# Layer 0 of a two-layer graph network: the normalised rows transposed by the DMA crossbar as two planes of 16 bits, and the head products placed among the next node tile's products

## The chip, the cores and the metric

The kernel runs on one core of a Trainium2 chip. A core has five engines, each with an instruction stream of its own that is executed in order: TensorE (PE, matmuls and transposes into PSUM), VectorE (DVE), ScalarE (ACT), GpSimd (POOL) and SyncE (SP). Here SP issues the loads and POOL the stores. Engines wait for each other through semaphores. The metric is the device time of one launch in microseconds, as the median of the runs; lower is better.

## The reference

There are 3327 nodes with 1024 features each, and a dense adjacency matrix of 3327 x 3327 with mostly zeros. Layer 0 quantises the normalised rows and the weights, multiplies them, and then multiplies by the adjacency matrix. Layer 1 is a graph attention with 8 heads of 64 features and a small dense network behind it. Both are residual. Cut to what matters here:

```python
h = jnp.maximum(_layernorm(x), 0.0)
x = x + _L0_gnn_ref(h, adj, ...)     # output = adj @ support_q, rescaled
h = jnp.maximum(_layernorm(x), 0.0)
Wh = jnp.einsum('nf,hfd->hnd', h, W)        # 1024 features -> 8 heads x 64
e_src = jnp.einsum('hnd,hd->hn', Wh, a1)
e_dst = jnp.einsum('hnd,hd->hn', Wh, a2)
e = jnp.where(adj > 0, leaky_relu(e_src[:, :, None] + e_dst[:, None, :], 0.2), NEG)
att = jax.nn.softmax(e, axis=-1)
x = x + mlp(elu(einsum('hnm,hmd->hnd', att, Wh)))
```

The change concerns the fourth line and the normalisation above it: the product of the normalised rows of `x` after layer 0 with the head weights `W`.

## The kernel before

The nodes are cut into 26 tiles of 128 (`T`). The kernel has four parts: the quantised product of layer 0 (`s_int`, one tile of 128 x 1024 for each node tile, all kept in SBUF), the adjacency product of layer 0 (lines 433 to 460), the attention, and the dense network.

The adjacency product is the part at hand. For each node tile `t` there are 104 matmuls of 128x128 by 128x512 (line 444): 26 column blocks `j`, two halves of the output, and two summands `hi` and `lo` of the adjacency block, which is split so that two rounded products add up to the exact one. The column blocks come in four parts of 7, 6, 7 and 6 (`PARTS`). `adjacency` (lines 172 to 189) loads a part (`at`, 3 buffers), makes `hi` on ScalarE (line 179) and `lo` on VectorE (line 183), each with 2 buffers, and the mask of non-zeros (`mk`, line 184). A part is asked for one part ahead of its products.

When a tile's products are done, ScalarE reads them out of PSUM (`y`, line 452), VectorE rescales them (line 453), adds the old rows (`xt`, line 454), and `normalised` computes mean and variance, then the inverse deviation (`inverse_std`, lines 127 to 137), and writes `(xt - mean) * r` to `y` (line 152). POOL stores `xt`.

`heads(t, h)` then works on the normalised tile: TensorE transposes its eight blocks of 128 x 128 (line 381), ScalarE copies them to `ht` with a ReLU (line 382), TensorE multiplies them by the head weights (line 385, eight float32 matmuls that show as sixteen in the trace), ScalarE copies the product (`wht`, line 387), VectorE forms the two attention terms `src` and `dst` (lines 392 and 393), TensorE transposes `src` (line 399), and ScalarE and VectorE build the features `ft`, `fw` and `dw`, which POOL stores for the attention. `heads` is called one tile late: after the products of tile `t` and its normalisation, the heads of tile `t - 1` are worked on, and the heads of the last two tiles follow the loop.

A scheduler sets the order of the instructions on each engine, moving them within what the data allow; `tc.keep_in_program_order` pins an instruction to where it is written. In the order that it made, the eight transposes of tile `t - 1` stand right behind the products of tile `t`, then five products of tile `t + 1`, then the head matmuls, ten products, the transpose of `src`, and the other 89 products. SP's queue holds the `at` loads, four to a tile, and one load of old rows `xt` (line 125). At the end of the part, the loads of the attention (masks, `f_even`, `dw`, `srow`) follow in the same queue.

Of the kernel before, what the change touches and what calls it, by code (L numbers as in the profile page):

```python
# [8 lines left out]
F32 = mybir.dt.float32  # L9
BF16 = mybir.dt.bfloat16  # L10
F32R = mybir.dt.float32r
U8 = mybir.dt.uint8
I8 = mybir.dt.int8
AF = mybir.ActivationFunctionType
ALU = mybir.AluOpType
# [4 lines left out]
P = 128  # L20
N = 3327
T = (N + P - 1) // P
NP = T * P
TH = T // 2
F = 1024
KF = F // P
# [9 lines left out]
EPS = 1e-5  # L36
# [23 lines left out]
def two_layer_kernel(  # L60
# [23 lines left out]
    nc = tc.nc  # L84
# [5 lines left out]
    ident = const.tile([P, P], F32, name="ident")  # L90
# [7 lines left out]
    x1_d = dram.tile([NP, F], F32, name="x1_d")  # L98
    mask_d = dram.tile([T, P, T, P], U8, name="mask_d")
    feat_d = dram.tile([T, NH, P, HW], F32, name="feat_d")  # L100
# [26 lines left out]
    def inverse_std(var, n, eps, tag):  # L127

        v, s, r, q = (small.tile([P, n], F32, tag=tag + c, name=tag + c) for c in "vsrq")
        nc.vector.tensor_scalar(v, var, eps, None, ALU.add)  # L130
        nc.scalar.activation(s, v, AF.Sqrt)
        nc.vector.reciprocal(r, s)
        nc.vector.tensor_tensor(q, v, r, ALU.mult)
        nc.vector.tensor_tensor(q, q, s, ALU.add)
        nc.vector.tensor_scalar(q, q, 0.5, None, ALU.mult)
        nc.vector.reciprocal(r, q)
        return r
# [7 lines left out]
    def normalised(dst, src):  # L145

        stats = small.tile([P, FC, 6], F32, tag="stats", name="stats")
        statistics(stats, src)
        mv = small.tile([P, 2], F32, tag="mv", name="mv")
        nc.vector.bn_aggr(mv, stats.rearrange("p c s -> p (c s)"))  # L150
        r = inverse_std(mv[:, 1:2], 1, EPS, "ln")
        nc.vector.tensor_scalar(dst, src, mv[:, 0:1], r, ALU.subtract, ALU.mult)

    def normaliser(mv, n, eps, factor, tag):

# [12 lines left out]
    with tc.tile_pool(name="wh", bufs=1, reuse_waits="tile") as whp, tc.tile_pool(  # L168
        name="at", bufs=2, reuse_waits="tile"
# [56 lines left out]
        with tc.tile_pool(name="s1", bufs=2, reuse_waits="tile") as s1, tc.tile_pool(  # L226
            name="s1_tp", bufs=2, space=PSUM, reuse_waits="tile"
# [81 lines left out]
            for c in range(FC):  # L309
                r = slice(c * 512, (c + 1) * 512)  # L310
# [16 lines left out]
            whead = whp.tile([P, KF, EMB], F32, name="whead")  # L327
# [43 lines left out]
        with tc.tile_pool(name="s2", bufs=2, reuse_waits="tile") as s2, tc.tile_pool(  # L371
            name="s2_tp", bufs=2, space=PSUM, reuse_waits="tile"
        ) as tp_ps, tc.tile_pool(name="s2_wh", bufs=2, space=PSUM, reuse_waits="tile") as wh_ps:

            def heads(t, h):
                ht = s2.tile([P, KF, P], F32, name="ht", bufs=1)
                for g in range(KF // 4):
                    tp = tp_ps.tile([P, 4, P], F32, tag="tp2", name="tp2")
                    for q in range(4):
                        k = 4 * g + q  # L380
                        nc.tensor.transpose(tp[:, q, :], h[:, k * P : (k + 1) * P], ident)
                    nc.scalar.activation(ht[:, 4 * g : 4 * g + 4, :], tp, AF.Relu)  # L382
                whm = wh_ps.tile([P, EMB], F32, name="whm")
                for k in range(KF):
                    nc.tensor.matmul(whm, ht[:, k, :], whead[:, k, :], start=(k == 0), stop=(k == KF - 1))  # L385
                wht = s2.tile([P, EMB], F32, name="wht", bufs=1)
                nc.scalar.copy(wht, whm)
                src = small.tile([P, NH], F32, name="src")
                dst = small.tile([P, NH], F32, name="dst")
                for a_t, e in ((a1_t, src), (a2_t, dst)):  # L390
                    prod = s2.tile([P, EMB], F32, name="prod", bufs=1)
                    nc.vector.tensor_tensor(prod, wht, a_t, ALU.mult)
                    nc.vector.tensor_reduce(
                        e, prod.rearrange("p (h d) -> p h d", d=HD), AX.X, ALU.add
                    )
                nc.vector.tensor_scalar(ndst[:, t], dst, -1.0, None, ALU.mult)
                nc.scalar.activation(ratio[:, t], src, AF.Exp, scale=1.0 - SLOPE)
                sp = tp_ps.tile([P, 4, P], F32, tag="tp2", name="sp")
                nc.tensor.transpose(sp[:NH, 0, :], src, ident)
                srct = s2.tile([NH, P], F32, name="srct")  # L400
                nc.scalar.copy(srct, sp[:NH, 0, :])
                for sub, d in zip(SUBS, src_d):
                    if t in sub:
                        nc.gpsimd.dma_start(d[:, (t - sub[0]) * P : (t - sub[0] + 1) * P], srct)

                ft = s2.tile([P, NH, 2, HC], F32, name="ft", bufs=1)
                wh3 = wht.rearrange("p (h d) -> p h d", d=HD)
                for q, slope in enumerate((1.0, SLOPE)):
                    nc.scalar.activation(ft[:, :, q, HD], dst, AF.Exp, scale=slope)
                    nc.vector.tensor_tensor(  # L410
                        ft[:, :, q, :HD], wh3, ft[:, :, q, HD:].to_broadcast([P, NH, HD]), ALU.mult
                    )
                fw = s2.tile([P, NH, 2, 2 * HC], F32R, name="fw", bufs=1)
                f2 = ft.rearrange("p h q c -> p h (q c)")
                nc.scalar.copy(fw[:, :, 0], f2)
                nc.vector.tensor_tensor(fw[:, :, 1], f2, fw[:, :, 0].bitcast(F32), ALU.subtract)

                dw = s2.tile([P, NPAIR, 2, 2, HC], F32R, name="dw", bufs=1)
                for q in range(2):
                    nc.scalar.copy(  # L420
                        dw[:, :, q],
                        fw[:, :, q, HC:].bitcast(F32).rearrange("p (g e) c -> p g e c", e=2),
                    )
                nc.gpsimd.dma_start(
                    feat_d[t].rearrange("h p c -> p h c"),
                    fw.bitcast(F32).rearrange("p h q c -> p h (q c)"),
                )
                nc.gpsimd.dma_start(
                    dsum_d[t].rearrange("g p c -> p g c"),
                    dw.bitcast(F32).rearrange("p g q e c -> p g (q e c)"),  # L430
                )

            before = None
            for t in range(T):
                xt = s2.tile([P, F], F32, name="xt2")
                load_rows(xt, x, t)
                mm = mm_ps.tile([P, F], F32, tag="mm", name="mm2")
                for js in PARTS:
                    hi, lo = part
                    part = next(columns, None)  # L440
                    for q, j in enumerate(js):
                        for which in (hi, lo):
                            for c in range(FC):
                                nc.tensor.matmul(  # L444
                                    mm[:, c * 512 : (c + 1) * 512],
                                    which[:, q, :],
                                    s_int[j][:, c * 512 : (c + 1) * 512],
                                    start=(j == 0 and which is hi),
                                    stop=(j == T - 1 and which is lo),
                                )  # L450
                y = s2.tile([P, F], F32, name="y")
                nc.scalar.activation(y, mm, AF.Copy, scale=r_asf)
                nc.vector.tensor_scalar(y, y, asf_t, sup_delta, ALU.mult, ALU.mult)
                nc.vector.tensor_tensor(xt, xt, y, ALU.add)
                nc.gpsimd.dma_start(x1_d[t * P : (t + 1) * P, :], xt)
                normalised(y, xt)
                if before is not None:
                    heads(*before)
                before = (t, y)
            heads(*before)  # L460
    supp.close()

# [23 lines left out]
    with tc.tile_pool(name="f1", bufs=1, reuse_waits="tile") as f1p, tc.tile_pool(  # L486
        name="sel", bufs=4, reuse_waits="tile"
    ) as selp, tc.tile_pool(name="srow", bufs=2, reuse_waits="tile") as srowp, tc.tile_pool(name="mf", bufs=2, reuse_waits="tile") as mfp, tc.tile_pool(
        name="md", bufs=2, reuse_waits="tile"
    ) as mdp, tc.tile_pool(name="s3", bufs=1, reuse_waits="tile") as s3, tc.tile_pool(  # L490
        name="s3_acc", bufs=7, space=PSUM, reuse_waits="tile"
# [142 lines left out]
        for i, (c, g, e, si) in enumerate(attends):  # L634
# [75 lines left out]
            h = 2 * g + e  # L710
            sub, mask = halves[c][si], masks[si]
            nb = len(sub)
            f = f_odd if e else f_even
            srow_next = load_src(i + 1) if i + 1 < len(attends) else None
            accs = [acc_ps.tile([P, HW], F32, tag="acc", name="acc") for _ in sub]
            for j in range(T):
                n = i * T + j
                k, m = divmod(n - 20, 2 * T)
# [41 lines left out]
    with tc.tile_pool(name="s4", bufs=2, reuse_waits="tile") as s4, tc.tile_pool(  # L760
        name="s4_ps", bufs=4, space=PSUM, reuse_waits="tile"
# [22 lines left out]
        for g, t0 in enumerate(range(0, T, 4)):  # L784
# [7 lines left out]
            else:  # L792
                enct = s4.tile([P, EMB // P, 512], F32, name="enct")
                for k in range(EMB // P):
                    tp = ps_p.tile([P, 512], F32, tag="ps", name="tp4")
# [8 lines left out]
            for q, t in enumerate(tiles):  # L804
                nc.vector.tensor_tensor(x1[:, q, :], x1[:, q, :], bb4, ALU.add)
                ps = o_ps.tile([P, F], F32, name="o")
                for c in range(FC):
                    for k in range(D3 // P):
# [4 lines left out]
                            start=(k == 0),  # L813
                            stop=(k == D3 // P - 1),
# [50 lines left out]
```

## Time and profile before

| | us |
|---|---|
| median of 3 runs | 2292.01 |
| lowest and highest | 2291.98, 2293.26 |
| the profiled execution, its time | 2293.44 |
| the profiled execution, its span | 2291.7 |
| adjacency product, from the first `y` to the last (170.9 to 957.5) | 786.6 |

The granted TensorE clock was 0.995 of full speed. Rows of the profile read thus: a group of instructions has its line, engine, operation, what it writes and reads, shapes and count, then the busy time of the group and the mean duration of one, then the idle time of the engine just before them and what ended it. Matmuls are pipelined, so their means overlap; the distance between two starts is the price of one. A row of a timeline has start, duration, and in brackets the idle time before it. A row of a stage has its busy time and instruction counts of PE, PEld (weight loads, beside PE), DVE, ACT and POOL, then the granted clock, the busy share of the DMA engines and GB/s. A row of DMA issues has the size and the median time from issue to landing.

### The profile page before, as it was taken

To read this page: it belongs to the slowest core of one execution; us is meant where nothing else is said; L and a number is where in the kernel's file an instruction comes from. 1 tells how busy PE (TensorE), PEld (TensorE's weight loads), DVE (VectorE), ACT (ScalarE), POOL (GpSimd) and SP (SyncE) were. 2 spreads that over 40 slices of the span, in tenths; PEclk is the share of its full clock that TensorE was granted. 3 is DMA by queue.
4 is the path that set the end of the run, shared out by engine and by line. 5 is a ranking of instruction groups with operands and counts; after the bars stand their busy time and mean duration, and the time that the engine had idled before them with its cause. 6 is when DMAs were issued, how large, how long until landed. Compare 5 with 4: busy or idle time off the path is not lost. (4 is left out here: it accounts for less than half of the span.)

```text
span 2291.7 us, 32041 instructions
## 1 busy us (share of the span) xinstructions
PE 2233.5 (97%) x12896; PEld 1785.0 (78%) x12896; DVE 1559.1 (68%) x2090; ACT 998.2 (44%) x1654; POOL 119.3 (5%) x173
## 2 busy tenths in 40 slices
PE   4999999999999999889999999999999999999999
PEld 2467777777777777579999999999999999744444
DVE  7845555555555555487999999999999999732211
ACT  4753333333333333346555555555555555411120
POOL 0000110111101111000000000000000000000000
PEclk9999999999999999999999999999999999999999
DMA  6324444444445444763324142654242422343311
GB/s 234 129 82 149 151 150 142 162 145 155 151 141 162 151 149 152 239 210 118 99 73 134 45 142 80 215 178 154 84 144 77 141 87 75 112 152 123 125 55 55
DMA packets 150301, 304.94 MB, mean 133 GB/s; under 512 B 10172, under 2 KB 91020, under 8 KB 150152
## 3 DMA queue, kind: packets, MB, share of 16 engines
q1 hardware_dynamic: 130248, 229.72, 30.3%
q0 software_dynamic: 19904, 73.17, 9.9%
q8 instruction: 101, 1.65, 0.3%
q14 instruction: 48, 0.39, 0.1%
HBM read 216.07 MB, written 86.79 MB: 132 GB/s over the span
## 5 line engine op out<-in xcount | busy, mean ns | idle before, releaser
L729 DVE SCALAR_TENSOR_TENSOR sel<-srow,ndst,mask 128x896 fp32r<-128x896 f32 (+1 forms) x832 | 864.1, 1079 | 54.4 <-PE acc L738 41.2
L539 PE MATMUL mps<-dw,mf 128*128 128x260 f32 x2704 | 453.3, 283 | 0.1
L444 PE MATMUL mm<-s_int,hi 128*128 128x512 f32 x1352 | 433.0, 399 | 0.0
L444 PE MATMUL mm<-s_int,lo 128*128 128x512 f32 x1352 | 421.6, 391 | 0.0
L738 PE MATMUL acc<-f_even,sel 128*128 128x260 f32 x2704 | 396.9, 284 | 1.4 <-DVE sel L729 1.1
L738 PE MATMUL acc<-f_odd,sel 128*128 128x260 f32 x2704 | 395.0, 286 | 0.0
L538 ACT CAST mf<-mask 128x1664 fp32r<-128x1664 uint8 x208 | 331.3, 1593 | 123.5 <-PE mps L539 100.2
L539 PEld LDWEIGHTS mps<-dw,mf 128*128 128x128 f32 x2704 | 377.7, 188 | 0.3 <-ACT part L543 0.3
L738 PEld LDWEIGHTS acc<-f_odd,sel 128*128 128x128 f32 x2704 | 353.4, 188 | 7.3 <-issue 3.1
L738 PEld LDWEIGHTS acc<-f_even,sel 128*128 128x128 f32 x2704 | 354.9, 188 | 5.4 <-DVE sel L729 2.8
L444 PEld LDWEIGHTS mm<-s_int,lo 128*128 128x128 f32 x1352 | 253.8, 188 | 57.6 <-issue 5.7
L444 PEld LDWEIGHTS mm<-s_int,hi 128*128 128x128 f32 x1352 | 252.1, 188 | 55.6 <-issue 5.7
L184 DVE TENSOR_SCALAR mk<-at 128x896 uint8<-128x896 f32 x104 | 61.7, 594 | 267.1 <-DMA at<-in_adj_t 266.1
L179 ACT CAST hi<-at 128x896 fp32r<-128x896 f32 x104 | 92.7, 891 | 328.8 <-PE mm L444 294.8
L385 PE MATMUL whm<-whead,ht 128*128 128x512 f32 x416 | 186.7, 602 | 0.8 <-ACT ht L382 0.8
L809 PE MATMUL o<-weights,h 128*128 128x512 f32 x416 | 179.7, 592 | 0.0
L809 PEld LDWEIGHTS o<-weights,h 128*128 128x128 f32 x416 | 79.0, 190 | 99.1 <-issue 99.0
L385 PEld LDWEIGHTS whm<-whead,ht 128*128 128x128 f32 x416 | 77.4, 191 | 98.0 <-issue 87.8
L183 DVE TENSOR_TENSOR lo<-at,hi 128x896 fp32r<-128x896 f32 x104 | 106.6, 1025 | 49.0 <-ACT hi L179 38.8
L543 ACT COPY part<-mps 128x260 f32<-128x260 f32 x104 | 39.3, 378 | 223.9 <-PE mps L539 223.9
L819 DVE TENSOR_TENSOR yo<-o,nodes 128x1024 f32<-128x1024 f32 (+1 forms) x27 | 31.8, 1182 | 139.2 <-PE o L809 139.2
L333 PE MATMUL mm<-w_int,xqt 128*128 128x512 bf16 x416 | 97.7, 386 | 10.2 <-DVE w_int L319 7.7
(136 smaller groups left out, 1567.8 us busy)
## 6 DMA issues: line engine op xcount, KB each, us to landing
feat_d<-fw POOLq DMA_DIRECT2D x26, 1040.0 KB, 5.3
f_even<-feat_d SPq DMA_DIRECT2D x7, 3380.0 KB, 13.1
f_odd<-feat_d SPq DMA_DIRECT2D x7, 3380.0 KB, 12.3
at<-in_adj_t SPq DMA_DIRECT2D x52, 448.0 KB, 4.2
at<-in_adj_t SPq DMA_DIRECT2D x52, 384.0 KB, 3.2
mask<-mask_d SPq DMA_DIRECT2D x39, 416.0 KB, 6.9
dw<-dsum_d SPq DMA_DIRECT2D x16, 910.0 KB, 8.9
dsum_d<-dw POOLq DMA_DIRECT2D x26, 520.0 KB, 6.5
```

The lines of the kernel that those rows point to most:

```text
L179: ins = nc.scalar.copy(hi, at)
L183: nc.vector.tensor_tensor(lo, at, hi.bitcast(F32), ALU.subtract)
L184: nc.vector.tensor_scalar(mk[:, r], at, 0.0, None, ALU.is_gt)
L333: nc.tensor.matmul(mm[:, c * 512 : (c + 1) * 512], xqts[t][:, k, :], w_int[:, k, c * 512 : (c + 1) * 512], start=(k == 0), stop=(k == KF - 1),
L385: nc.tensor.matmul(whm, ht[:, k, :], whead[:, k, :], start=(k == 0), stop=(k == KF - 1))
L444: nc.tensor.matmul(mm[:, c * 512 : (c + 1) * 512], which[:, q, :], s_int[j][:, c * 512 : (c + 1) * 512], start=(j == 0 and which is hi), s ...
L538: nc.scalar.copy(mf, mask[:, j : j + TH, :])
L539: nc.tensor.matmul(ps, mf[:, j % TH, :], dw[:, j, :], start=(j == 0), stop=(j == T - 1))
L543: nc.scalar.copy(part[:, i % 7], ps.rearrange("p (q c) -> p q c", q=2))
L729: nc.vector.scalar_tensor_tensor(sel[:, :nb], srow[:, :nb], ndst[:, j, h : h + 1], mask[:, :, j, :], ALU.is_gt, ALU.mult,)
L738: nc.tensor.matmul(accs[b], sel[:, b, :], f[:, j, :], start=(j == 0), stop=(j == T - 1))
L809: nc.tensor.matmul(ps[:, c * 512 : (c + 1) * 512], h3[:, k, q * P : (q + 1) * P], w4[:, k, c * 512 : (c + 1) * 512], start=(k == 0), stop= ...
```

## The change

Four things are changed.

- Tiles 0 to 24 are transposed by a DMA on SP's queue. ScalarE first copies `y` into two planes of 16 bits (`yh`: all lower halves of the float32 words, then all upper halves), the DMA transposes 128 rows by 2048 columns into sixteen blocks (`yht`), and ScalarE copies the planes back into float32 words (`ht`). The last tile is transposed by TensorE as before.
- The transposition is asked for right after the tile's normalisation.
- The heads of tile `t - 1` are called within the products of tile `t`, after column block 16, and their first matmul is pinned there.
- `normalised` writes `max(xt - mean, 0)` and hands the inverse deviation `r` on. As `r` is positive and one number for each row, it is multiplied in later, where `heads` reads its product out of PSUM (`wht`).

`y` has one buffer instead of two.

```diff
+U16 = mybir.dt.uint16
@@ normalised
-        r = inverse_std(mv[:, 1:2], 1, EPS, "ln")
-        nc.vector.tensor_scalar(dst, src, mv[:, 0:1], r, ALU.subtract, ALU.mult)
+        nc.vector.tensor_scalar(dst, src, mv[:, 0:1], 0.0, ALU.subtract, ALU.max)
+        return inverse_std(mv[:, 1:2], 1, EPS, "ln")
@@ adjacency product
-            def heads(t, h):
+            def halves_of_words(words):
+
+                return words.bitcast(U16).rearrange("p (n two) -> p two n", two=2)
+
+            def transposed_by_dma(y):
+
+                yh = s2.tile([P, 2, F], U16, name="yh", bufs=1)
+                nc.scalar.copy(yh, halves_of_words(y))
+                yht = s2.tile([P, 2 * KF, P], U16, name="yht", bufs=1)
+                nc.sync.dma_start_transpose(yht, yh.rearrange("p two f -> p (two f)"))
+                ht = s2.tile([P, KF, P], F32, name="ht", bufs=1)
+                nc.scalar.copy(
+                    halves_of_words(ht.rearrange("p k i -> p (k i)")),
+                    yht.rearrange("p (two k) i -> p two (k i)", two=2),
+                )
+                return ht
+
+            def transposed_by_tensor(y):
                 ht = s2.tile([P, KF, P], F32, name="ht", bufs=1)
                 for g in range(KF // 4):
                     tp = tp_ps.tile([P, 4, P], F32, tag="tp2", name="tp2")
                     for q in range(4):
                         k = 4 * g + q
-                        nc.tensor.transpose(tp[:, q, :], h[:, k * P : (k + 1) * P], ident)
-                    nc.scalar.activation(ht[:, 4 * g : 4 * g + 4, :], tp, AF.Relu)
+                        nc.tensor.transpose(tp[:, q, :], y[:, k * P : (k + 1) * P], ident)
+                    nc.scalar.copy(ht[:, 4 * g : 4 * g + 4, :], tp)
+                return ht
+
+            def heads(t, ht, r):
                 whm = wh_ps.tile([P, EMB], F32, name="whm")
                 for k in range(KF):
-                    nc.tensor.matmul(whm, ht[:, k, :], whead[:, k, :], start=(k == 0), stop=(k == KF - 1))
+                    ins = nc.tensor.matmul(
+                        whm, ht[:, k, :], whead[:, k, :], start=(k == 0), stop=(k == KF - 1)
+                    )
+                    if k == 0:
+                        tc.keep_in_program_order(ins)
                 wht = s2.tile([P, EMB], F32, name="wht", bufs=1)
-                nc.scalar.copy(wht, whm)
+                nc.scalar.activation(wht, whm, AF.Copy, scale=r)
@@ the loop over node tiles
+                        if j == 16 and before is not None:
+                            heads(*before)
-                y = s2.tile([P, F], F32, name="y")
+                y = s2.tile([P, F], F32, name="y", bufs=1)
...
-                normalised(y, xt)
-                if before is not None:
-                    heads(*before)
-                before = (t, y)
+                r = normalised(y, xt)
+                before = t, (transposed_by_tensor if t == T - 1 else transposed_by_dma)(y), r
             heads(*before)
```

## The prediction

> **What bounds the kernel now.** I read the page first (which engine is full), then busy time by stage, then the groups of the stage that the diff touches, then its timelines.
>
> ```profile
> PE 2233.5 (97%) x12896; PEld 1785.0 (78%) x12896; DVE 1559.1 (68%) x2090; ACT 998.2 (44%) x1654; POOL 119.3 (5%) x173
> ...
> 234.00:957.00 723.00, 723.00 (x2940) 530.59 (x2939) 382.38 (x627) 268.87 (x407) 76.06 (x113) 1.00 0.47 153
> 957.00:990.00 33.00, 19.63 (x56) 9.43 (x54) 16.44 (x28) 10.66 (x19) 2.79 (x4) 0.84 1.00 348
> ```
>
> In the second part of layer 0 (234 to 957 us) TensorE is busy for all 723 us; VectorE 382, ScalarE 269, DMA engines at 0.47. Only PE's work, or a wait on PE, counts there. The 33 us at its end are different: PE busy for 20, DMA share 1.00 at 348 GB/s.
>
> ```profile
> L385 PE MATMUL whm<-whead,ht 128*128 128x512 f32 x416 | 186.7, 602 | 0.8 <-ACT ht L382 0.8
> L381 PE MATMUL tp<-ident,y 128*128 128x128 f32 x208 | 27.8, 278 | 0.3 <-DVE y L152 0.3
> ```
>
> The 208 transposes (8 for each of 26 node tiles) hold PE for 27.8 us; 200 of them go. Means overlap, so their price is better read from starts, PE's timeline of one tile:
>
> ```profile
> 511.61 0.62 PE L444 MATMUL mm<-s_int,lo 128*128 128x512 f32 x2
> 512.07 1.03 PE L381 MATMUL tp<-ident,y 128*128 128x128 f32 x8
> 512.86 0.71 PE L444 MATMUL mm<-s_int,hi 128*128 128x512 f32 x2
> ...
> 513.86 0.39 PE L444 MATMUL mm<-s_int,hi 128*128 128x512 f32 x1
> 514.20 7.13 PE L385 MATMUL whm<-whead,ht 128*128 128x512 f32 x16
> 520.77 0.79 PE L444 MATMUL mm<-s_int,hi 128*128 128x512 f32 x1
> ```
>
> Products start every 0.227 us (two in 0.46). The eight transposes take 512.86 - 512.07 = 0.79; the step from the last product to the heads is 0.34 instead of 0.23, PE waiting 0.11 for `ht`; and the 16 head matmuls (0.43 a start) contain one more such wait of about 0.1. Sum 1.0 us a tile. The period comes from the starts of `y` (ScalarE's timeline):
>
> ```profile
> 170.89 1.11 ACT L452 ACTIVATE y<-mm,r_asf 128x1024 f32<-128x1024 f32 x1
> ...
> 194.46 1.11 ACT L452 ACTIVATE y<-mm,r_asf 128x1024 f32<-128x1024 f32 x1
> ...
> 512.54 1.11 ACT L452 ACTIVATE y<-mm,r_asf 128x1024 f32<-128x1024 f32 x1
> ...
> 544.36 1.11 ACT L452 ACTIVATE y<-mm,r_asf 128x1024 f32<-128x1024 f32 x1
> ```
>
> A tile with heads in it is 31.82 us; tile 1, which has none before the change, 23.57.
>
> [...]
>
> **The change part by part.** S is the start of a tile's first product; it lies 0.47 us before `y` (512.07 to 512.54).
>
> *Removed.* 1.0 us of PE in each of 25 tiles; the two 0.59 us reads of the transposed PSUM on ScalarE (hidden). A tile with heads becomes 31.8 - 1.0 = 30.8, plus a wait w if `ht` is late.
>
> *Moved.* In the program's order the 16 head matmuls stand after 68 of the tile's 104 products, so PE reaches them at S + 68 x 0.2265 = S + 15.4. They now belong to the previous tile, so tile 1 has heads too, and only the last tile's heads remain behind the loop. Loop before: 786.6 us (170.9 to 957.5). After: 25 x 30.8 = 770 + 25w. That is -16.6 + 25w.
>
> *The new chain, from PE's end to `ht`.* VectorE's part of it, in the second tile shown (S = 543.9):
>
> ```profile
> 545.51 0.81 DVE L453 TENSOR_SCALAR y<-y,every,sup_delta 128x1024 f32<-128x1024 f32 x1
> 546.35 1.23 DVE L454 TENSOR_TENSOR xt<-xt,y 128x1024 f32<-128x1024 f32 x1
> 547.61 1.29 DVE L141 BATCH_NORM_STATS2 stats<-xt 128x6 f32<-128x512 f32 x2
> ...
> 549.71 0.20 DVE L150 BATCH_NORM_AGGREGATE mv<-stats 128x2 f32<-128x12 f32 x1
> ```
>
> There the first `y` starts at S+1.6. In the new order one mask comparison more (0.56) stands ahead of it: S+2.1. Then 0.84 + 1.26 + 1.32, another comparison 0.55, 0.24, and the subtract-and-max at the price of the old normalisation, 0.81: 5.0, so `y` is ready at S+7.1. The inverse deviation is off this path, since it now scales `wht`. On ScalarE `hi` of part 2 stands before `yh`; it waits for PE's part 0 (S + 28 x 0.227 = 6.3 at the latest) and takes 0.95, so it is out of the way at about 7.1. `yh` has 2048 elements a partition: 1040 take 1.06 us (`fw`) and 520 take 0.63 (`dw`), that is 0.83 ns an element and 0.2 fixed: 1.9. [...] It ends at S+9.0.
>
> *The DMA.* SP's order is `xt` of the next tile, the transpose, then the next `at` loads: behind the waiting transpose stand only loads for the next tile, wanted over 10 us later, and ahead of it a 512 KB load that starts about S+7.5. The trace's nearest transfers:
>
> ```profile
> xt<-in_x SPq DMA_DIRECT2D x25, 512.0 KB, 3.2
> enc_d<-ht POOLq DMA_DIRECT2D x16, 224.0 KB, 3.1
> enc_d<-ht POOLq DMA_DIRECT2D x16, 192.0 KB, 2.8
> ```
>
> If as fast as a regular 512 KB, X = 3.2 us. If it goes by pieces of 256 bytes, as `enc_d` does (7 x 128 pieces in 3.1, 6 x 128 in 2.8: 0.3 per 128), 2048 pieces give 3.1 + 9 x 0.3 = 5.8. [...] I take 4.5, the middle of the two values from this trace. `ht` is another 1.9 us of ScalarE, with `hi` of part 3 ahead of it, which is done at about S+12.9, before the data. So `ht` ends at S + 9.0 + 4.5 + 1.9 + 0.3 for hand-overs = S+15.7: w = 15.7 - 15.4 = 0.3, in all 7.5 us. Behind `ht` on ScalarE wait only the heads' own work and then `hi` of the next tile's part 0. In the trace `ft` ends 4.4 us after the last head product (520.8 to 525.2); `hi` (0.95) and `lo` (1.1) make 6.5, while PE has 36 products (8.2 us) left: covered by 1.7 us.
>
> *The end of the stage.* Before, the heads of tile 24 and 25 both follow the loop, and PE stands for the transpose of `src`:
>
> ```profile
> PE sp L399 <- DVE src L393: 12.1, 2, 9.9
> ```
>
> VectorE was waiting for loads with four `sel` queued ahead of `prod`. From the last `y` (957.5) to the first attention product (989.4) is 31.9 us. After: `y` ready 5.6 us after the last product, tensor transposes and copies to 7.3, heads to 14.3; `srow`, behind two more `dw` pieces but started 7 us earlier against the loop's end, lands at about 11.4, four `sel` to 15.9, `prod` and its sum to 17.5, attention at 18. That is -14; I take -12, for the transpose of tile 24 now shares the queue with three mask loads (416 KB each). If the stretch stays bound by its DMA, as the share of 1.00 allows, it is only -3.
>
> Sum: -16.6 + 7.5 - 12 = -21. The profiled run took 2293.4 us with a span of 2291.7, the median is 2292.0; the difference of 0.06% is below anything argued here. 2292 - 21 = 2271.
>
> **The rivals.** With w = 0 the whole is worth 28.6 us, 1.14 a tile. So the change turns into a loss where the transposing DMA takes over 4.5 - 0.3 + 1.14 = 5.35 us, or the two copies together take 0.84 us more than I took at 4.5.
>
> *A. In time or nearly so* (X from 3.2 to 5.2): 2263 to 2288, forecast 2271. For it: [...] DMA engines at 0.47. Against: pieces of 256 bytes, and `xt` just ahead in the queue.
>
> *B. The transposing DMA is late, and PE waits for `ht` in each tile; slower.* One mechanism: PE executes in order, so the whole of X beyond 5.35 is lost 25 times over. By the pieces' price of 5.8, w = 1.6: 40 - 28.6 = +11, 2303. At 8 us, w = 3.8: +66, 2358. [...] For it: [...] the `enc_d` rows. Against: nothing in this trace moves 512 KB so slowly without a queue ahead of it.
>
> *C. It cancels* (X about 5.2 to 5.5): 2292.
>
> *D. The loop gains, the end doesn't*: -16.6 + 7.5 - 3 = -12, 2280; it lies within A. That the transposes stay on PE is excluded: in the new order only the last tile's eight are left.
>
> **How the numbers follow.** A (with D) 0.55, C 0.05, B 0.40, of which 0.25 up to X = 8.7 and 0.15 above. What this kernel's measurement can tell from no change is about 0.2%, 4.6 us. Faster 0.55, same 0.05, slower 0.40. A's own range is 2260 to 2288. The range on record reaches from 2258 (no wait, the end at its best, and 0.1 us a tile for the rounding of 1.0) to 2375 (X = 8.7), leaving out the far end of B.
>
> **What would show it.** Right: `y` to `y` at 30.8 to 31.2 us; `yht` landing within 5 us of its issue; head matmuls preceded by less than 0.5 us of PE idle; first attention product about 18 us after the last `y`. Wrong: PE idle before `whm` put down to ACT `ht`, of over 1.1 us a tile; `yh` or `ht` well above 1.9 us; PE waiting at the start of a tile for `hi` or `lo`. A landing time over 5.35 us alone would turn the sign.

## The result, and the profile after

| | before | after |
|---|---|---|
| median | 2292.11 us (4 runs) | 2397.49 us (4 runs) |
| lowest and highest | 2291.98, 2293.26 | 2387.61, 2399.82 |
| the profiled execution: time, span | 2293.44, 2291.7 | 2395.86, 2393.8 |
| granted clock over the span | 0.995 | 0.975 |
| adjacency product, first `y` to last | 786.6 | 902.2 |
| last `y` to the first attention product | 31.8 | 18.9 |
| from there to the end of the span | 1302.3 | 1302.3 |

The ratio is 1.045, with an interval of 1.042 to 1.048: slower, where faster had been forecast. All of it lies in the adjacency product: +115.6 us there, -13.0 at its end, nothing behind. ScalarE's timeline has the two ends of the loop (start, duration):

```profile
170.48 1.11 ACT L479 ACTIVATE y<-mm,r_asf 128x1024 f32<-128x1024 f32 x1
...
1072.65 1.11 ACT L479 ACTIVATE y<-mm,r_asf 128x1024 f32<-128x1024 f32 x1
```

25 periods in 902.2 us are 36.1 us each; before, a tile with heads took 31.8, and 30.8 plus a wait of 0.3 was forecast. The groups of the changed instructions, PE's and ScalarE's:

```profile
L406 PE MATMUL whm<-whead,ht 128*128 128x512 f32 x416 | 228.7, 713 | 86.3 <-ACT ht L387 86.3
L399 PE MATMUL tp<-ident,y 128*128 128x128 f32 x8 | 2.0, 428 | 5.8 <-DVE lnv L131 5.8
L387 ACT COPY ht<-yht 128x2048 uint16<-128x2048 uint16 x25 | 61.6, 2466 | 59.5 <-DMA yht<-yh 59.5
L383 ACT COPY yh<-y 128x2048 uint16<-128x2048 uint16 x25 | 47.5, 1899 | 71.7 <-DVE y L152 71.7
```

200 transposes are gone, as intended. In their place PE stands for 86.3 us ahead of the head products, waiting for ScalarE's copy `ht`, and the head products themselves are busy for 228.7 us instead of 186.7. The transposing DMA is not what is slow (the view of the tile `yht`: durations of the issue in ns, min/median/max, then the times to landing):

```profile
L385 SPq DMA_TRANSPOSE yht<-yh x25: 1798/1942/3491, 178.9 to 1049.5; - x25
...
DMA to landing us min/median/max: 4.2/4.3/6.6
```

So PE waits, but the transfer takes 4.3 us in the median, no more than the 4.5 that were taken for it. Most of the time must be lost before it. One tile shows where; its first product starts at S = 574.31. First POOL's timeline (DMA issues; start, duration, and in brackets the wait before):

```profile
573.77 0.93 POOL L449 DMA_DIRECT2D feat_d<-fw  x1 [4.24 <-DVE fw L441]
574.69 0.77 POOL L453 DMA_DIRECT2D dsum_d<-dw  x1
578.62 0.55 POOL L482 DMA_DIRECT2D x_d<-xt  x1 [3.15 <-DVE xt L481]
```

SP's:

```profile
584.09 0.33 SPq L126 DMA_DIRECT2D xt<-in_x  x1
586.03 3.14 SPq L385 DMA_TRANSPOSE yht<-yh  x1
```

VectorE's:

```profile
578.35 1.29 DVE L142 BATCH_NORM_STATS2 stats<-xt 128x6 f32<-128x512 f32 x2
582.53 0.63 DVE L185 TENSOR_SCALAR mk<-at 128x896 uint8<-128x896 f32 x1 [2.89 <-DMA at<-in_adj_t]
583.08 0.20 DVE L151 BATCH_NORM_AGGREGATE mv<-stats 128x2 f32<-128x12 f32 x1
583.31 0.75 DVE L152 TENSOR_SCALAR y<-xt,mv 128x1024 f32<-128x1024 f32 x1
```

ScalarE's:

```profile
584.10 1.90 ACT L383 COPY yh<-y 128x2048 uint16<-128x2048 uint16 x1 [2.88 <-DVE y L152]
...
591.22 2.46 ACT L387 COPY ht<-yht 128x2048 uint16<-128x2048 uint16 x1 [2.98 <-DMA yht<-yh]
```

PE's:

```profile
589.14 0.61 PE L469 MATMUL mm<-s_int,lo 128*128 128x512 f32 x2
593.73 9.94 PE L406 MATMUL whm<-whead,ht 128*128 128x512 f32 x16 [3.97 <-ACT ht L387]
603.11 1.02 PE L469 MATMUL mm<-s_int,hi 128*128 128x512 f32 x2
```

Between the statistics and the mean VectorE has a mask comparison `mk` in its queue, and waits 2.89 us for the adjacency load `at` that it reads. This load is issued at S+1.6, while the two stores of the previous tile's heads (`feat_d` 1040 KB, `dsum_d` 520 KB, issued at S-0.5 and S+0.4) are on the DMA engines, and lands 6.5 us later; the load at the same place of the tile of before landed after 3.9. There the heads' stores went out late in the tile, at S+17.9 (S = 512.07, POOL's timeline of before):

```profile
529.95 0.93 POOL L424 DMA_DIRECT2D feat_d<-fw  x1 [5.02 <-DVE fw L416]
```

`y` is ready at S+9.8, forecast S+7.1. From there the chain runs nearly as forecast: `yh` 1.90, DMA 5.17 (this tile is slower than the median of 4.3), `ht` 2.46, PE at S+19.4 instead of S+15.4. And the 16 head products then take 603.11 - 593.73 = 9.4 us instead of the 6.57 (514.20 to 520.77) of before.

The stages view in slices of about 8 us, for this tile and for the tile of before that the prediction used. Columns: PE, PEld, DVE, ACT and POOL busy, granted clock, DMA share, GB/s. Before, from S = 512.07:

```profile
512.07:520.07 8.00, 8.00 (x28) 4.39 (x27) 6.08 (x13) 4.04 (x6) 1.10 (x2) 1.00 0.52 177
520.07:528.07 8.00, 8.00 (x34) 5.84 (x34) 5.98 (x11) 4.29 (x8) 0.53 (x1) 1.00 0.19 67
528.07:536.07 8.00, 8.00 (x37) 6.64 (x36) 3.11 (x4) 2.38 (x4) 1.70 (x2) 1.00 0.74 237
536.07:543.90 7.83, 7.83 (x37) 6.41 (x36) 1.83 (x3) 1.23 (x2) 0.00 (x0) 1.00 0.40 123
```

After, from S = 574.31:

```profile
574.31:582.31 8.00, 8.00 (x37) 6.63 (x36) 4.66 (x6) 2.53 (x3) 2.25 (x4) 1.00 0.92 303
582.31:590.31 8.00, 7.45 (x33) 5.82 (x31) 4.23 (x11) 4.11 (x4) 0.00 (x0) 1.00 0.89 220
590.31:598.31 8.00, 4.58 (x6) 2.00 (x7) 1.19 (x2) 2.46 (x1) 0.00 (x0) 0.64 0.34 109
598.31:606.31 8.00, 8.00 (x25) 4.30 (x24) 1.81 (x3) 2.28 (x4) 0.00 (x0) 0.93 0.00 0
606.31:612.08 5.77, 5.77 (x27) 4.76 (x26) 4.66 (x7) 3.79 (x8) 1.07 (x2) 1.00 0.19 51
```

Read the DMA column downwards. Before, the third slice had the most (0.74): there the heads' stores went out. After, they sit in the first slice, and the first two are at 0.92 and 0.89, just where the chain to `ht` needs its loads and its transfer; from 594 to 606 the DMA engines are nearly empty. The mean share over the loop is 0.49, as before (0.47), and tells nothing of this.

The clock column is the second finding. The same view around the wait:

```profile
592.30:593.70 1.40, 0.00 (x0) 0.00 (x0) 0.02 (x1) 1.38 (x1) 0.00 (x0) 0.60 0.87 353
593.70:598.70 5.00, 4.97 (x6) 2.19 (x7) 1.17 (x2) 0.00 (x0) 0.00 (x0) 0.50 0.01 4
598.70:603.10 4.40, 4.40 (x11) 1.88 (x10) 0.00 (x0) 0.00 (x0) 0.00 (x0) 0.92 0.00 0
```

After the wait of 3.97 us PE runs for 5 us at a granted clock of 0.50, and then for 4.4 us at 0.92; in the last 1.4 us of the wait it is at 0.60 already. That the lower clock belongs to the waits is shown by e6 below: there PE waits 0.9 us in all, the clock over the loop is 1.00, and the head products are busy for 185.2 us, against 186.7 before the change and 228.7 here. What makes the clock fall and come back, and after how long, was not shown; how long the waits were that had slow head products behind them is in the last section.

Together: 86.3 us of waiting and about 43 us of slow head products (228.7 against the 185.2 of a later version that doesn't wait) are about 130 of the 132 us by which the loop is longer than its 770 without waits.

### The profile page after: what moved, and what is told of

Read it like the earlier page. It is cut to its first block, busy times and chain, and to the rows that moved or that the text cites. A ratio compares the mean times of both kernels' runs of the same rounds, so it can differ in the third digit from the quotient of the medians.

```text
span 2393.8 us, 31681 instructions
## 1 busy us (share of the span) xinstructions
PE 2254.0 (94%) x12684; PEld 1779.3 (74%) x12696; DVE 1548.7 (65%) x2090; ACT 1082.5 (45%) x1656; POOL 118.5 (5%) x173
## 5 line engine op out<-in xcount | busy, mean ns | idle before, releaser
L469 PE MATMUL mm<-s_int,hi 128*128 128x512 f32 x1352 | 427.0, 397 | 0.0
L406 PE MATMUL whm<-whead,ht 128*128 128x512 f32 x416 | 228.7, 713 | 86.3 <-ACT ht L387 86.3
L406 PEld LDWEIGHTS whm<-whead,ht 128*128 128x128 f32 x416 | 93.1, 230 | 211.1 <-issue 114.1
L417 DVE TENSOR_TENSOR prod<-wht,a_t 128x512 f32<-128x512 f32 x52 | 36.0, 692 | 225.8 <-ACT wht L412 224.9
L412 ACT ACTIVATE wht<-whm,lnr 128x512 f32<-128x512 f32 x26 | 17.9, 688 | 230.3 <-PE whm L406 230.3
```

The costliest lines, as they stand in the source:

```text
L406: ins = nc.tensor.matmul(whm, ht[:, k, :], whead[:, k, :], start=(k == 0), stop=(k == KF - 1))
L469: nc.tensor.matmul(mm[:, c * 512 : (c + 1) * 512], which[:, q, :], s_int[j][:, c * 512 : (c + 1) * 512], start=(j == 0 and which is hi), s ...
```

## The experiments

These lines allow two theories. The mask theory says that the loss is the mask comparison alone, which stands ahead of the mean and waits for a late load. The store theory says that the heads' stores, moved into the first microseconds of the tile, fill the DMA engines, and that the comparison is only one of several things that wait. Each expectation names its own theories. A third question was whether the placing of the heads in the products costs anything by itself. All of them are compared with before; "loop" is the adjacency product from the first `y` to the last, and "PE idle" is summed over all tiles:

| run | median, us | ratio (95%) | loop | PE idle before `whm` |
|---|---|---|---|---|
| changed kernel | 2397.49 | 1.045 (1.042 to 1.048) | 902.2 | 86.3 |
| e1: mask made from `hi` | 2394.67 | 1.0433 (1.0407 to 1.0459) | 904.3 | 91.4 |
| e4: heads after block 18 | 2299.38 | 1.0032 (1.0020 to 1.0044) | 809.3 | 26.8 |
| e3: e1 and e4 together | 2317.50 | 1.0111 (1.0096 to 1.0126) | 826.7 | 40.0 |
| e2: TensorE transposes, heads moved | 2284.71 | 0.9967 (0.9954 to 0.9980) | 792.3 | 0.0 |
| e5: stores late, on SP's queue | 2293.09 | 1.0007 (0.9999 to 1.0016) | 800.3 | 24.2 |
| e8: stores late, on POOL's queue | 2303.37 | 1.0043 (1.0028 to 1.0058) | 809.5 | 30.0 |
| e9: stores early, on SP's queue | 2418.64 | 1.0544 (1.0526 to 1.0561) | 924.0 | 90.1 |
| e6: e5 and heads after block 18 | 2262.45 | 0.9872 (0.9856 to 0.9889) | 769.7 | 0.9 |
| e7: heads two tiles late | 2283.68 | 0.9966 (0.9953 to 0.9979) | 778.8 | 0.2 |

**e1: the mask comparison doesn't wait for the load.**

```diff
-            nc.vector.tensor_scalar(mk[:, r], at, 0.0, None, ALU.is_gt)
+            nc.vector.tensor_scalar(mk[:, r], hi.bitcast(F32), 0.0, None, ALU.is_gt)
```

> The changed kernel with one edit: the comparison mk reads hi in place of at, so on VectorE it can no longer stand before the mean and variance and wait there for the load of the next tile's part 0. Theory A (the heads come late mainly because y waits behind that comparison, whose load lands 6.5 us after its issue beside the stores of feat_d and dsum_d): y is ready at S+6.5 to 7.2 instead of S+9.8 (S: the tile's first product), yh ends at about 9.1, the transpose lands at 13.4, ht ends at 15.9, PE waits under 1.0 us before the heads, the 16 head products take 6.54 us from first to last start instead of 8 to 9.6, a tile takes 31.2 to 31.6 us instead of 36.4, and the time is 2270 to 2290. Rival B (the transposing DMA and its copies are too long by themselves): the wait stays above 3 us and the time above 2370. Rival C (the lower granted clock comes from something other than the waits): the wait shrinks, but head products still take over 8 us in most tiles, 2310 to 2340.

Nothing came of it: 2394.67. The corresponding tile starts at S = 570.10. VectorE's timeline:

```profile
575.84 0.75 DVE L152 TENSOR_SCALAR y<-xt,mv 128x1024 f32<-128x1024 f32 x1
```

SP's:

```profile
580.92 0.33 SPq L126 DMA_DIRECT2D xt<-in_x  x1
581.35 3.94 SPq L385 DMA_TRANSPOSE yht<-yh  x1
```

ScalarE's:

```profile
577.84 1.89 ACT L383 COPY yh<-y 128x2048 uint16<-128x2048 uint16 x1
588.27 2.46 ACT L387 COPY ht<-yht 128x2048 uint16<-128x2048 uint16 x1 [6.47 <-DMA yht<-yh]
```

`y` is ready at S+6.5, 3.3 us earlier than in the changed kernel, and `yh` at S+9.6. But SP issues the transposing DMA only at S+11.25, behind the `xt` load of the next tile, which waits for the store `x_d` of the rows in its buffer; that landed at S+10.81. (In other tiles SP has the transposition ahead of `xt`, and issues it at S+9.2.) And then the data take 6.9 us, the median over the tiles too, against 4.3. The wait has moved from VectorE into SP's queue and the DMA engines, to the same end. The mask theory falls: without the comparison's wait the loss stays. That both are late for one shared reason is what e5 and e8 show below.

**e4 and e3: the heads after column block 18 instead of 16**, the second with the edit of e1.

```diff
-                        if j == 16 and before is not None:
+                        if j == 18 and before is not None:
                             heads(*before)
```

> The changed kernel with the heads after column block 18 in place of 16 and nothing else. In the order that results, the comparison of the next tile's part 0 no longer stands between the sums and the mean on VectorE. Theory A: y ready at about S+7.5, no wait before the heads, 30.8 to 31.3 us a tile, 2260 to 2280. If y still waits until S+9.8, ht ends at S+18.7 and PE waits 1.4 us: 32.3 us a tile, about 2300. Rival B (transpose and copies are too long by themselves): over 2340.

> As e1_mask_hi, with the heads after column block 18 in place of 16, 1.8 us later. Theory A: ht (S+15.9) is there before PE comes to the heads (S+17.2), no wait, 30.8 us a tile, 2258 to 2270: faster than both kernels by over 1%. Rival D (the heads' own followers, hi and lo of the next tile's part 0, then come late): PE waits at the start of a tile instead, 0.5 to 2 us, 2275 to 2310.

Two column blocks are 8 products, 1.8 us, yet e4 gains 98 us of the 105 lost. The later place also gives other orders: in the tile looked at (S = 724.14) VectorE has the comparison behind `y`, SP has the transposition ahead of `xt`, and the stores go out at S+2.1. So `y` is ready at S+6.9, the transposing DMA issued at S+8.9, and what is left of the stores' effect is its landing time, 6.3 us in the median. PE's wait is then 0.6 us in most tiles, and no wait below 2.2 us was followed by slow head products (last section): against the changed kernel 59.5 us of waiting go (86.3 to 26.8) and 33.8 us of slow head products (228.7 to 194.9), together 93, as many as the loop is shorter (92.9). With e1's edit on top it is 18 us slower, not faster: PE's waits add up to 40.0 us, and in the tiles with the longest of them the transposing DMA landed after 7.5 to 10.3 us, against 6.2 in the median. Why it is later in these tiles stays open.

**e2: the heads moved, but transposed by TensorE** (after column block 12, pinned there; their products after 16 as in the changed kernel; no transposing DMA).

```diff
+                        if j == 12 and before is not None:
+                            ht = transposed_by_tensor(before[1])
                         if j == 16 and before is not None:
-                            heads(*before)
+                            heads(before[0], ht, before[2])
...
-                before = t, (transposed_by_tensor if t == T - 1 else transposed_by_dma)(y), r
+                before = t, y, r
...
```

> The other part of the change alone: the heads among the next tile's products as in the changed kernel (products after column block 16), but the transposes by TensorE, after column block 12, and no transposing DMA and no planes. y may be late as in the changed kernel (S+9.8), which is still before S+11.8 where PE comes to the transposes. Theory A: no wait of PE, 31.6 to 31.8 us a tile, 25 tiles with heads in place of 24 and one without, and an end that is 12 us shorter: 2280 to 2290. If moving the heads costs PE by itself (their stores beside the loads delay hi or lo), 2300 or more.

2284.71, 7 us below before. The move of the heads costs nothing by itself: the stores go out as early as in the changed kernel (S-0.5), and `y` is as late (S+9.8 in the median), but PE comes to the transposes only at S+11.7, `ht` is then copied from PSUM, and PE has no wait ahead of the head products. So the early stores cost time only together with the new chain.

**e5, e8 and e9: the time of the stores, and their queue.** In e5 `heads` hands its two stores back, and they are issued by SP behind the next tile's transposing DMA. This changes two things at once, the time and the queue, so two more runs take them apart: in e8 POOL issues the stores, after it has read one column of the next tile's `ht`; in e9 SP issues them, and nothing holds them back. (`crossing` is a list of the transposing DMAs.)

```diff
+                def store(queue):
+                    queue.dma_start(
+                        feat_d[t].rearrange("h p c -> p h c"),
+                        fw.bitcast(F32).rearrange("p h q c -> p h (q c)"),
+                    )
...
+                return store
...
@@ e5, behind the transposition of the tile
+                    with tc.issue_after(crossing[-1].ins):
+                        store(nc.sync)
@@ e8, in place of these two lines
+                    ins = nc.gpsimd.tensor_copy(seen, before[1][:, 0, 0:1])
+                    with tc.issue_after(ins.ins):
+                        store(nc.gpsimd)
@@ e9, the changed kernel with this alone, and the same for dsum_d
-                nc.gpsimd.dma_start(
+                nc.sync.dma_start(
                     feat_d[t].rearrange("h p c -> p h c"),
```

> The changed kernel, heads after column block 16 as there, with only the stores of feat_d and dsum_d (1.5 MB a tile) moved: SP issues them behind the next tile's transposing DMA instead of POOL at the start of the next tile. VectorE's order is that of the changed kernel, the comparison of part 0 still ahead of the mean. Theory E (the moved heads put their stores into the first 8 us of the next tile, where they hold all DMA engines and delay first the at load that the comparison waits for, then the transpose): the at load lands in 3 to 4 us, y is ready at about S+7.1, the transpose is issued at S+9 and lands within 4.5 us, ht ends at S+15.9, PE waits 0.6 us and not 3.5 to 6, no head products at the lower clock, 31.2 to 31.6 us a tile, 2270 to 2285. Rival B' (the transpose itself is slower when issued early, whatever the other traffic): it lands at S+15 as in the runs before, PE waits over 2 us, above 2310.

> The two stores of the heads stay on POOL's queue, as in the changed kernel, but POOL first reads one word of `ht` into a scratch column, so they are issued about S+16 instead of S+0. The run before moved them in time and to SP's queue at once; this one moves them in time alone. Theory 1 (when they are issued is what costs): `y` at S+6.9, the transposing DMA issued at S+8.9 and landing in 4.3 to 4.8, PE idle 0.5 to 1 us before the heads: 2278 to 2295 us. Theory 2 (the queue matters[...]): over 2340 us.

> The two stores of the heads are moved to SP's queue and nothing holds them back: they go out when SP reaches them in its order, behind two or three loads of the adjacency block and ahead of the next tile's first part, its `xt` and its transposition. Theory 1 (time of issue): as late as the changed kernel, since the transposition now stands behind both stores in the same queue as well: 2350 to 2420 us. Theory 2 (queue): as with SP's late stores, 2285 to 2300 us.

In e5 VectorE keeps the order of the changed kernel, comparison ahead of the mean; but its timeline (S = 589.32) has no wait there any more:

```profile
593.37 1.29 DVE L142 BATCH_NORM_STATS2 stats<-xt 128x6 f32<-128x512 f32 x2
594.57 0.61 DVE L185 TENSOR_SCALAR mk<-at 128x896 uint8<-128x896 f32 x1
595.10 0.20 DVE L151 BATCH_NORM_AGGREGATE mv<-stats 128x2 f32<-128x12 f32 x1
```

PE's group of head products in e5:

```profile
L408 PE MATMUL whm<-whead,ht 128*128 128x512 f32 x416 | 188.6, 607 | 24.2 <-ACT ht L389 24.2
```

in e8:

```profile
L408 PE MATMUL whm<-whead,ht 128*128 128x512 f32 x416 | 192.6, 617 | 30.0 <-ACT ht L389 30.0
```

in e9, where the stores are issued between S-0.8 and S+2.1 (in the last tile up to S+2.7):

```profile
L406 PE MATMUL whm<-whead,ht 128*128 128x512 f32 x416 | 238.9, 739 | 90.1 <-ACT ht L387 90.1
```

Late stores take 94 us (POOL) and 104 us (SP) away; early stores cost as much on SP's queue as on POOL's (somewhat more: 2418.64). The time of their issue decides, not the queue. In e9 the loss takes the path of e1: `y` is ready at S+6.4 in the median, but the store `x_d` lands only at S+10.7, `xt` waits for it, and SP issues the transposition behind `xt` at S+11.2. Both late versions miss their expectation by 8 us, though, since PE still waits about 1 us in each tile (24.2 and 30.0 us over 25): in e5 `y` is ready at S+6.8, the transposing DMA issued at S+8.7, landed after 4.8 us in the median, and `ht` takes 2.49, so `ht` is there at S+16.1, while PE comes at S+15.3. In e8 the end of the stage is longer too (22.4 us from the last `y` to the first attention product instead of 18.9): `srow` lands 15.5 us after its issue there, in e5 4.7. The later stores are the likely cause, but no run tests it.

**e6: late stores and the heads after block 18**, both edits as above.

> As e5_store_late with the heads after column block 18. Theory E: ht is there (S+15.9) before PE comes to the heads (S+17.2): no wait, 30.8 to 31.0 us a tile, 2257 to 2268, faster than both kernels. Rival B': as in the run with the heads after block 18 alone, 2299.

2262.45 us (2261.58 to 2263.05), the fastest of all and 1.3% below before. The group of the head products:

```profile
L408 PE MATMUL whm<-whead,ht 128*128 128x512 f32 x416 | 185.2, 599 | 0.9 <-ACT ht L389 0.9
```

ScalarE's timeline at the two ends of the loop:

```profile
170.06 1.11 ACT L484 ACTIVATE y<-mm,r_asf 128x1024 f32<-128x1024 f32 x1
...
939.75 1.11 ACT L484 ACTIVATE y<-mm,r_asf 128x1024 f32<-128x1024 f32 x1
```

769.7 us for 25 tiles, 30.8 each: the prediction's figure without any wait. One tile in slices (S = 570.79), against the two tables above:

```profile
570.79:578.79 8.00, 8.00 (x37) 6.63 (x36) 7.71 (x11) 5.35 (x7) 1.10 (x2) 1.00 0.48 157
578.79:586.79 8.00, 8.00 (x37) 6.61 (x36) 2.42 (x8) 5.26 (x5) 0.00 (x0) 1.00 0.97 271
586.79:594.79 8.00, 8.00 (x23) 3.98 (x22) 1.19 (x2) 0.43 (x1) 0.00 (x0) 1.00 0.61 188
594.79:601.51 6.72, 6.72 (x31) 5.32 (x30) 5.42 (x9) 3.97 (x8) 0.53 (x1) 1.00 0.22 59
```

The first slice is at 0.48 again, the stores fill the second and third behind the transposing DMA, and PE is busy throughout at full clock.

**e7: the stores as in the changed kernel, but the heads of two tiles before, after column block 6.** Here `ht` has most of a tile to spare.

```diff
-                        if j == 16 and before is not None:
-                            heads(*before)
+                        if j == 6 and len(before) > 1:
+                            heads(*before.pop(0))
...
```

> The changed kernel with the heads of tile t - 2 (not t - 1) among the products of tile t, after column block 6. The transpose then has more than half a tile of slack, and the stores fall at about S+18 to S+25, where the DMA engines were idle. Theory E: no wait before the heads whenever the transpose lands, 30.8 to 31.0 us a tile; the heads of two tiles follow the loop as before the change, so the end gains nothing: 23.6 + 24 x 30.9 = 765 against 787, that is 2265 to 2275. If the planes' copies on ScalarE or the crossbar disturb PE in another way, over 2290.

```profile
L424 PE MATMUL sp<-ident,src 128*8 128x128 f32 x26 | 7.2, 277 | 29.3 <-DVE src L418 29.1
```

The wait for `ht` is gone (0.2 us) and a new one is there: PE stands 29.3 us ahead of the transpose of `src`. Of these, 12.1 lie behind the loop, as before the change; the 17.2 in the loop are new, since VectorE reaches `prod` and `src` later than PE needs them at this place. In one tile VectorE stood 3.57 us just ahead of `prod`, in a mask comparison that waited for its load `at`. With two tiles' heads left behind the loop (29.1 us to the first attention product) it makes 2283.68, 9 us above the upper end of what was expected.

## Why the prediction was wrong, point by point

- *What bounds the kernel: PE in the loop, only its work or its waits count.* Right, and the reason for the size of the miss.
- *1.0 us of PE a tile for the transposes, 30.8 us without a wait.* Right: 30.8 in e6.
- *`y` ready at S+7.1.* Right only where the comparison ahead of the mean doesn't wait: S+6.8 in e5, which has the same order on VectorE; S+9.8 in the changed kernel, in the median as in the tile shown. The sum counted the comparison itself (0.55) and not the load that it waits for.
- *`yh` 1.9 us.* Right: 1.90. *`ht` another 1.9.* Too small: 2.47, or 2.49 to 2.51 in e5 and e6; the same elements, but the steps of four bytes are on the side that is written.
- *X = 4.5 us.* Right: 4.3 in the median, 4.8 and 4.9 in e5 and e6; 6.2 to 6.9 where the transfer meets the early stores (e1, e3, e4). It lies between the two values taken from the trace of before, and both miss it: 512 KB by a regular load took 3.2 us, a quarter less than 4.3; and the 5.8 was an estimate that took the `enc_d` stores for pieces of 256 bytes, while of the 64 packets of one of them (192 KB) 48 have 2 KB or more. In the changed kernel's trace the stretch of the transposing DMA shown above (586.0 to 591.2) has 2180 packets, 2096 of them under 512 bytes.
- *Behind the waiting transpose stand only loads for the next tile, and ahead of it one 512 KB load; 7.5 us of waits.* This is the step that failed. The queues were searched for what stands behind and beside the transposing DMA in SP's order, with `xt` as its only company, and the moved heads' two stores were not moved along: POOL's `feat_d` and `dsum_d` went from S+18 into the first microseconds of the tile. In the changed kernel they delay `at`, and with it `mk`, the mean and `y`: in the medians over the tiles `y` is 2.7 us later than forecast, `ht` 0.6 us longer and the transfer 0.2 us shorter, so that `ht` is there at S+18.7 and not at S+15.7. Where `y` doesn't wait (e1, e9), they delay `x_d`, and with it `xt` and SP's turn at the transposition, and in e1, e3 and e4 the transfer itself. PE's waits are 86.3 us instead of 7.5. That these stores are the cause is shown by e8, which moves them in time and adds only a small copy on POOL, by e5, and by e9, where they are early on the other queue; that the comparison alone isn't, by e1.
- *-12 us at the end of the stage.* Right in size: 31.8 to 18.9, -13.0. But not by the links of the sum, which had `srow` and the four `sel` end last, at 15.9 after the last `y`. `srow` landed at 6.0 and the `sel` were done at 10.6; the head products ended last, at 16.5 instead of 14.3, slow after a wait of 5.78 us. That the two errors nearly cancel is luck.

```profile
1078.27 1.97 PE L399 MATMUL tp<-ident,y 128*128 128x128 f32 x8 [5.78 <-DVE lnv L131]
1080.06 9.13 PE L406 MATMUL whm<-whead,ht 128*128 128x512 f32 x16
```

- *Rival B, PE waiting for `ht` in each tile.* The place was right and the mechanism wrong: it was to come from a transposing DMA over 5.35 us, and came with one of 4.3. Its price was taken as the wait alone, and the half clock after a longer wait was left out; that is about 43 of the 132 us.

In the prediction's own sum: 777.5 us of loop became 902.2. Of the 124.7 between them 79 are waits beyond the 7.5 allowed and 43 are slow head products; 2 to 3 are not assigned.

One thing stays open: e5's loop is 31 us longer than e6's. PE's waits (24.2 against 0.9 us) and head products (188.6 against 185.2) make 27 of them. In two tiles PE is idle for over 2 us, and what made these later than the others was not followed.

## What to carry to other kernels

When a block of work is moved, move its DMA issues too, and lay them out over one period against the loads that the critical chain needs in that period; a mean DMA share of 0.49 hid 16 us at about 0.9 in the tile shown. Removing the wait that the trace names may only move it, if what it waits for is late for a shared reason: ask what else stands behind the same resource first. And a new wait on TensorE is to be priced with the clock that it loses, not by its length alone: here about 43 us of slow head products came on top of 86.3 us of waiting.

## What the runs showed of the hardware

- *Half clock after short waits.* In the loops of the kernels with the transposing DMA there are 176 tiles in which PE waited for `ht`, measured from the start of the last product to the start of the first head product (0.23 without a wait). Of 87 waits below 2.2 us none slowed the 16 head products (6.54 us from the first start to the last), of 38 between 2.2 and 3.7 us 26 did, and of 51 above 3.7 all but one did (7.9 to 9.6 us; the exception is a wait of 3.88 in e9). In the changed kernel alone it is none of 1, 7 of 12 and 12 of 12. Waits of like length go both ways: behind one of 2.48 us in e5 the head products took 8.26 us up to the next product, behind one of 3.61 in the changed kernel 6.57, as before the change. What decides between them was not shown.
- *Sixteen blocks in one transposing DMA.* 128 rows by 2048 columns of 16 bits take 4.2 us from issue to landing at best, and the issue holds SP's queue for 1.8 to 3.5 us in the changed kernel and up to 7.1 in e3, so that the loads behind it start later: in the tile shown it was issued at 586.03 and held the queue for 3.14 us, and the next `at` load went out at 589.61.
- *Copies of 16 bits in steps of four bytes.* On ScalarE 2048 elements a partition take 1.90 us when they are read so, and 2.47 when they are written so.
